# The router's sigmoid as ScalarE's own function, in place of an exponential, an addition and a reciprocal

## The chip, the cores and the metric

The kernel runs on one core of a Trainium2 chip. The metric is the device time of one execution in microseconds (us), as the median of the runs shown. The engines have short names in the profile: PE is TensorE (PEld its weight loads), DVE is VectorE, ACT is ScalarE, POOL is GpSimd, SP is SyncE, which here mostly issues DMAs.

## The reference

The input x has 16 rows of 256 time steps and 256 channels, 4096 tokens in all. First, spikes from a cumulative sum are added to it; then a mixture of experts with one shared expert is applied, with a residual. Cut to what matters:

```python
rates = relu(x) * 0.001
c  = cond[:, None, :] + cumsum(rates, axis=1)
x1 = x + (floor(c) - previous floor(c)) / 0.001      # a spike adds 1000

shared = (silu(xf @ w1) * (xf @ w3)) @ w2            # 256 -> 512 -> 256
s = sigmoid(concat([xf, tf]) @ router_W)             # tokens x 8 experts
_, topk_idx = top_k(s + router_bias, 2)
s_sel = take_along_axis(s, topk_idx)
gates = s_sel / (s_sel.sum() + 1e-9)
routed = sum over the two chosen experts of gates * (gelu(xf @ W1e) @ W2e)
out = x1 + (shared + routed) / 3
```

All arithmetic of weight is in fp32. The router's sigmoid `s` is used twice: to choose the two experts of each token, and for their gates.

## The kernel before

The 4096 tokens are cut into 8 chunks (`NCHUNK`) of 512 tokens (`N`), four sub-tiles (`J`) of 128 each. The kernel has three stages.

**Stage 1, by chunk.** For each chunk, `elementwise(i)` turns the input with PE transposes (tile `pt`), takes rates and a copy on ACT (L282, L291), and runs the cumulative sum on DVE (the scan at L306, sums at L316 to L321), the start value and the rounding on ACT (L334, L343), and the floor, difference and addition on DVE (L358 to L378). That gives the tile `x1`. One chunk later, `route(i)` computes the router of that chunk: 8 small matmuls into `pl` (L426), an addition on DVE (`lt`, L435), one transpose on PE into `pn` (L438), then the sigmoid: an exponential on ACT into the small tile `ex` (L442), an addition of 1 (L444) and a reciprocal (L445) on DVE into `sig`. About a dozen DVE operations on 128 x 32 elements follow: the bias, the best expert, the second best, and the sum `hot` of both choices (L447 to L470). PE counts with `hot` how many tokens went to each expert before (the tile `pr`, L475 to L480), then transposes `x1` back (`px`, L496); ACT copies that into the rows `x1t` (L497), DVE computes the target rows (`row`, `mine`, `at`, `at_i`, L502 to L509), and POOL scatters the rows to the expert regions in DRAM with 8 indirect DMAs (L513).

**The shared expert** is a stream of matmuls that fills PE in all stages: `shared_hidden` makes the tiles `ph` (L536), of which a pair gives one Silu on ACT (`as`, L546) and one product on DVE (`hs`, L547). The pool of `ph` has three buffers, so a fourth tile can be begun only when the Silu or the product has read the tile three before it. `shared_out` makes `pa` (L563) and adds it to `x1t` on DVE (L574). The helper `unit(n)` issues the next n tiles of this stream.

**Stage 2, by block.** After the last chunk, the rows are sorted by expert in DRAM. `run_blocks` takes 67 blocks (`MOST`) of 128 rows, loads each, turns it on DVE (L832), multiplies by the expert's weights on PE (`phe` L859, `py` L881) with a Gelu and a copy on ACT, and scatters the result on POOL (L890). Four further blocks run only if the counts need more than 67. **Stage 3** finishes the shared expert and combines.

**What sets the order.** Each engine works through its instructions in order. In the first and the last chunk's part, and in stages 2 and 3, regions marked `tc.manual_schedule` keep the order of the program on the engines they name. Between them, in the loop that runs `route(i - 1)` beside `elementwise(i)` for chunks 2 to 7, and for the router of chunk 0, the order on PE, DVE and ACT is chosen when the kernel is built, from the dependencies and the builder's own costs; so an edit in `route` also decides what stands around it. ACT's functions come in tables: an `ACT_TABLE_LOAD` stands in the instruction order wherever the next function isn't in the table that is active. After the first load, Relu, Identity and the copies have none of their own here; Silu, Gelu and the exponential do.

Of the kernel before, what the change touches and what calls it, by code (L numbers as in the profile page):

```python
# [16 lines left out]
AF = mybir.ActivationFunctionType  # L17
ALU = mybir.AluOpType
# [20 lines left out]
def kernel(  # L39
# [23 lines left out]
    nc = tc.nc  # L63
    B, T, D = x.shape
    HS = w1.shape[1]
    E, _, HE = w1e.shape
# [346 lines left out]
    def route(i):  # L413
        x1, x1t = x1s[i], x1ts[i]

        def small(tag, shape=(P, J, E), dt=F32):
            return rt.tile(list(shape), dt, tag=tag, name=f"{tag}_{i}")
# [18 lines left out]
        yield  # L436
        pn = p_t.tile([P, J, 32], F32, tag="pt", name=f"pn_{i}")
        nc.tensor.transpose(pn.rearrange("p j e -> p (j e)"), lt, ident)  # L438

        s = sig[:, ts(i, J), :]  # L440
        ex = small("ex")
        nc.scalar.activation(ex, pn[:, :, :E], AF.Exp, scale=-1.0)  # L442
        yield
        nc.vector.tensor_scalar(ex, ex, 1.0, None, ALU.add)  # L444
        nc.vector.reciprocal(s, ex)  # L445
        sel = small("sel")
        nc.vector.tensor_tensor(sel, s, rb[:, None, :].to_broadcast([P, J, E]), ALU.add)  # L447

# [214 lines left out]


    ro, nxt = route(0), elementwise(2)
    next(ro)
    next(ro)
# [17 lines left out]
    for i in range(2, NCHUNK):  # L685
        ro = route(i - 1)
        nxt = elementwise(i + 1) if i + 1 < NCHUNK else iter(())
        next(ro)
        next(el, None)
        unit()  # L690
        next(ro)
        next(el, None)
        next(ro)
        next(el, None)
        next(ro)
        unit()
        next(ro)
        next(el, None)
        next(ro)
        next(nxt, None)  # L700
        unit(1 + (i > 3 and i % 3 != 2) + (i == NCHUNK - 1))
        next(ro)
        next(el, None)
        next(ro)
        next(el, None)
        if i <= E // 2:
            load_experts(i - 1)
        el = nxt
    last = ctx.enter_context(ExitStack())
    last.enter_context(tc.manual_schedule(engines={PE, DVE, ACT}))  # L710
    nc.vector.tensor_copy(bidx, bidx_i)
    ro = route(NCHUNK - 1)
    next(ro)
    unit(0.5)
# [341 lines left out]
```

## Time and profile before

| what | value |
|---|---|
| median of the three runs | 335.84 us (335.32 to 845.69) |
| profiled execution, its own time | 334.36 us |
| its span, first to last instruction | 332.6 us |
| PE busy | 315.9 us, 95% of the span |
| DVE busy | 228.4 us, 69% |
| POOL busy | 164.8 us, 50% |
| ACT busy | 137.9 us, 41% |
| ACT table loads | 16: one at L282, 8 at L546, 6 at L442, one at L867, 1283 ns each |
| granted TensorE clock | 1.000 |

The span is shorter than the execution's own time by 1.76 us, which lie before the first and after the last instruction. The shares are averages over the three stages; stage 1 ends at about 142 us, where the last chunk's router is done, and there DVE is far busier than its average says. A line of the profile's groups gives the source line, the engine, the operation, the tile written and the tiles read, the count, the busy time with the mean of one in ns, and then the idle time of the engine just before, with what ended it.

### The profile page before, as it was taken

The page shows a single profiled execution, that of the slowest core. Times are in us where ns is not written, and L with a number is a line of the kernel's source. Part 1 is how long each engine was busy: PE and PEld are TensorE (multiplying, and loading weights), DVE is VectorE, ACT ScalarE, POOL GpSimd, SP SyncE. Part 2 cuts the span into 40 slices and gives each one's busy share as a digit, 9 for nine tenths or more (in the row PEclk, how much of TensorE's full clock was granted, in tenths as well). Part 3 has the DMA queues.
Part 4 walks back from the last instruction along what each step waited for, and adds up shares of the span by engine and source line. Part 5 has one row for each costly group of instructions (what it writes and reads, how often), then busy time and mean ns, then how long its engine had stood idle before and what let it go on. Part 6 is the DMA issues. An engine that isn't in the chain of part 4 may idle for free. (4 is left out here: it accounts for less than half of the span.)

```text
span 332.6 us, 6544 instructions
## 1 busy us (share of the span) xinstructions
PE 315.9 (95%) x1674; PEld 233.6 (70%) x1674; DVE 228.4 (69%) x656; ACT 137.9 (41%) x287; POOL 164.8 (50%) x197
## 2 busy tenths in 40 slices
PE   3799998999989999999999999999999999999996
PEld 2577644547545744746699999999999999465484
DVE  4777979999999997551477745554555552089993
ACT  4537385645675363040234344344444444301100
POOL 6000274787478688763035555555554655223220
PEclk9999999999999999999999999999999999999999
DMA  6999633242222212254446666666666762399933
GB/s 169 270 219 203 157 114 99 85 141 101 79 81 91 74 65 83 103 180 120 79 99 147 155 156 147 155 154 129 146 155 141 173 146 81 123 338 409 408 153 126
DMA packets 62533, 50.34 MB, mean 151 GB/s; under 512 B 42606, under 2 KB 52863, under 8 KB 62496
## 3 DMA queue, kind: packets, MB, share of 16 engines
q1 hardware_dynamic: 42240, 26.19, 32.7%
q0 software_dynamic: 7456, 20.86, 17.0%
q10 hardware_dynamic: 12800, 2.88, 5.2%
q8 instruction: 14, 0.23, 0.3%
q14 instruction: 23, 0.19, 0.2%
HBM read 27.44 MB, written 22.84 MB: 151 GB/s over the span
## 5 line engine op out<-in xcount | busy, mean ns | idle before, releaser
L536 PE MATMUL ph<-x,w_sb 128*128 128x512 f32 (+1 forms) x288 | 118.8, 559 | 4.8 <-DVE x L378 4.1
L890 POOL DMA_INDIRECT ys<-yb,to x67 | 66.1, 987 | 66.7 <-ACT yb L889 56.1
L513 POOL DMA_INDIRECT xs<-x1t,at_i x64 | 78.7, 1230 | 38.8 <-ACT xt L291 18.7
L536 PEld LDWEIGHTS ph<-x,w_sb 128*128 128x128 f32 x288 | 53.8, 195 | 53.2 <-issue 42.0
L859 PEld LDWEIGHTS phe<-xbt,w1e 128*128 128x128 f32 x536 | 70.3, 191 | 4.7 <-ACT hbt L867 0.9
L859 PE MATMUL phe<-xbt,w1e 128*128 128x128 f32 x536 | 70.7, 275 | 0.7 <-DVE xbt L832 0.7
L881 PE MATMUL py<-we,hbt 128*128 x268 | 68.8, 380 | 0.0
L827 DVE COPY w1e<-we 128x512 f32 x67 | 28.8, 430 | 45.2 <-PE phe L859 44.7
L563 PE MATMUL pa<-w_sb,hs 128*128 128x256 f32 x256 | 57.7, 380 | 0.0
L563 PEld LDWEIGHTS pa<-w_sb,hs 128*128 128x128 f32 x256 | 48.2, 190 | 8.9 <-issue 2.8
L881 PEld LDWEIGHTS py<-we,hbt 128*128 128x128 f32 x268 | 45.9, 191 | 3.5
L546 ACT ACTIVATE as<-ph 128x512 f32<-128x512 f32 (+1 forms) x36 | 19.9, 553 | 63.9 <-PE ph L536 54.1
L867 ACT ACTIVATE hbt<-phe 128x256 f32<-128x256 f32 x67 | 25.7, 383 | 45.2 <-PE phe L859 36.1
L547 DVE TENSOR_TENSOR hs<-as,ph 128x512 f32<-128x512 f32 (+1 forms) x36 | 22.4, 622 | 27.6 <-PE ph L536 21.4
L889 ACT COPY yb<-py 128x256 f32<-128x256 f32 x67 | 24.9, 372 | 22.7 <-PE py L881 21.8
L832 DVE STREAM_TRANSPOSE xbt<-xb 128x256 f32<-128x256 f32 x67 | 29.2, 436 | 0.0
L306 DVE TENSOR_TENSOR_SCAN tb<-keep,rates 128x1024 f32<-128x1024 f32 (+2 forms) x10 | 18.6, 1859 | 1.6 <-ACT rates L282 1.5
L497 ACT COPY x1t<-px 128x512 f32<-128x512 f32 x16 | 8.6, 591 | 25.1 <-PE px L496 25.1
L334 ACT ACTIVATE ta<-ta,cond_t 128x256 f32<-128x256 f32 x32 | 14.1, 498 | 7.9 <-DVE ta L321 7.0
L589 POOL DMA_DIRECT2D out_dram<-yc x8 | 5.8, 728 | 22.7 <-DVE yc L997 14.3
L463 POOL COPY x1t<-first 128x16 f32<-128x16 f32 x8 | 4.1, 516 | 22.6 <-DVE first L456 22.6
L574 DVE SCALAR_TENSOR_TENSOR x1t<-pa,x1t 128x512 f32<-128x512 f32 x14 | 9.6, 684 | 7.3 <-PE pa L563 7.3
(135 smaller groups left out, 264.5 us busy)
## 6 DMA issues: line engine op xcount, KB each, us to landing
xb<-xs SPq DMA_DIRECT2D x184, 33.0 KB
yc<-ys SPq DMA_DIRECT2D x8, 512.0 KB
we<-ys SPq DMA_DIRECT2D x8, 512.0 KB
xn<-in_x_dram SPq DMA_DIRECT2D x7, 512.0 KB
xb<-xs ACTq DMA_DIRECT2D x84, 33.0 KB
we<-in_L_cond_W1e_dram SPq DMA_DIRECT2D x8, 256.0 KB
we<-in_L_cond_W2e_dram SPq DMA_DIRECT2D x8, 256.0 KB
out_dram<-yc POOLq DMA_DIRECT2D x8, 256.0 KB, 6.2
```

The costliest lines, as they stand in the source:

```text
L513: nc.gpsimd.indirect_dma_start(out=xs_w[(i * J + j) * TOPK + q][:, :], out_offset=bass.IndirectOffsetOnAxis(ap=at_i[:, q, j : j + 1], axis=0),
L536: nc.tensor.matmul(ph, lhsT=w[:, k, ts(u, P)], rhs=x1[:, k, cols], start=(k == 0), stop=(k == KD - 1),)
L546: nc.scalar.activation(act, ps[0], AF.Silu)
L547: nc.vector.tensor_tensor(ht[:, u, cols], act, ps[1], ALU.mult)
L563: nc.tensor.matmul(pa[:, q, :], lhsT=ht[:, s, ts(n * h + q, P)], rhs=w2_sb[:, s, :], start=(s == 0), stop=(s == KS - 1),)
L827: nc.vector.tensor_copy(w, we[:, bass.ds(off, KD * HE)])
L832: nc.vector.transpose(xt.rearrange("p g k r -> p g (k r)"), block[b].pop("xb")[:, :, :FQ])
L859: nc.tensor.matmul(ph[:, m, :].rearrange("p (g r) -> p g r", r=Q), lhsT=w[:, k, ts(m, P)], rhs=xt[:, :, k, :], start=(k == 0), stop=(k == ...
L867: nc.scalar.activation(ht, ph, AF.Gelu)
L881: nc.tensor.matmul(py, lhsT=ht[:, k, :], rhs=we[:, bass.ds(off + KD * HE + k * D, D)], start=(k == 0), stop=(k == KH - 1),)
L889: nc.scalar.copy(yb, py)
L890: nc.gpsimd.indirect_dma_start(out=ys_w[b][:, :], out_offset=bass.IndirectOffsetOnAxis(ap=to[:, b : b + 1], axis=0), in_=yb, in_offset=Non ...
```

## The change

In `route`, the exponential with scale -1 into the small tile `ex`, the addition of 1 and the reciprocal are taken out. One ACT instruction with the function Sigmoid reads `pn` and writes the chunk's part of `sig`. The bias addition that follows on DVE then waits for ACT where it waited for the reciprocal. The `yield`, at which the router's steps are cut for interleaving, stands behind the ACT instruction as before. Lines below L446 move up by four.

```diff
         pn = p_t.tile([P, J, 32], F32, tag="pt", name=f"pn_{i}")
         nc.tensor.transpose(pn.rearrange("p j e -> p (j e)"), lt, ident)
-
         s = sig[:, ts(i, J), :]
-        ex = small("ex")
-        nc.scalar.activation(ex, pn[:, :, :E], AF.Exp, scale=-1.0)
-        yield
-        nc.vector.tensor_scalar(ex, ex, 1.0, None, ALU.add)
-        nc.vector.reciprocal(s, ex)
+        nc.scalar.activation(s, pn[:, :, :E], AF.Sigmoid)
+        yield
         sel = small("sel")
         nc.vector.tensor_tensor(sel, s, rb[:, None, :].to_broadcast([P, J, E]), ALU.add)
```

## The prediction

> **What bounds the kernel now.** I read the engines' busy time first, then the busy time by stretches of 20 us, then what PE waits for. The page's first lines:
>
> ```profile
> span 332.6 us, 6544 instructions
> ...
> PE 315.9 (95%) x1674; PEld 233.6 (70%) x1674; DVE 228.4 (69%) x656; ACT 137.9 (41%) x287; POOL 164.8 (50%) x197
> ```
>
> PE leaves 332.6 - 315.9 = 16.7 us free in the whole span, so no edit off PE can bring more than 5%. Where that time lies is seen in the view by stretches (length, then busy us of PE, PEld, DVE, ACT, POOL, each with its count; then clock and DMA):
>
> ```profile
> 20.00:40.00 20.00, 19.68 (x138) 14.95 (x137) 17.07 (x46) 11.46 (x23) 1.15 (x2) 1.00 0.94 173
> 40.00:60.00 20.00, 18.89 (x78) 9.01 (x77) 17.55 (x46) 13.39 (x21) 13.32 (x11) 1.00 0.37 124
> 60.00:80.00 20.00, 20.00 (x87) 11.18 (x86) 18.92 (x55) 12.02 (x22) 16.07 (x14) 1.00 0.35 115
> 80.00:100.00 20.00, 18.46 (x102) 10.95 (x100) 19.51 (x56) 11.86 (x22) 12.99 (x10) 1.00 0.24 80
> 100.00:120.00 20.00, 19.60 (x104) 12.57 (x104) 19.53 (x49) 9.82 (x17) 14.86 (x13) 1.00 0.21 75
> 120.00:140.00 20.00, 19.45 (x88) 11.86 (x87) 14.99 (x50) 6.87 (x12) 15.76 (x16) 1.00 0.25 90
> ...
> 200.00:220.00 20.00, 20.00 (x139) 18.84 (x138) 10.68 (x35) 8.55 (x23) 11.25 (x12) 1.00 0.66 149
> ```
>
> The router works only in the stretches from 20 to about 142 us. There DVE is up to 98% busy and PE idle for 0.32 + 1.11 + 0 + 1.54 + 0.40 + 0.55 = 3.92 us. From 180 to 280 us PE has no free time, so whatever is gained or lost in stage 1 shifts the rest as it stands. The waits of PE itself (who waited for whom: total us, times, longest):
>
> ```profile
> PE ph L536 <- DVE x L378: 4.1, 2, 3.6
> PE pt L275 <- DMA xn<-in_x_dram: 3.9, 1, 3.9
> PE pr L475 <- DVE hot L470: 2.9, 5, 0.9
> ```
>
> The first two are the start, before any router. The third is the end of the router's chain: `pr` waits for `hot`, five times. By the timeline these are chunk 1 at 51.86 us (0.90), chunk 3 at 83.68 (0.43), chunk 4 at 94.44 (0.63), chunk 5 at 112.67 (0.40) and chunk 6 at 123.43 (0.55): 2.91 us of the 3.92. So the chain that the edit shortens ends in a wait of the bounding engine, but in short waits.
>
> **The change part by part.** The groups that it removes or replaces, and, from the timeline, the chunk that shows the spacing best (start, duration, engine, line):
>
> ```profile
> L445 DVE RECIPROCAL sig<-ex 128x32 f32<-128x32 f32 x8 | 2.8, 351 | 0.2
> L444 DVE TENSOR_SCALAR ex<-ex 128x32 f32<-128x32 f32 x8 | 1.4, 175 | 5.6 <-ACT ex L442 5.6
> L442 ACT ACTIVATE ex<-pn 128x32 f32<-128x32 f32 x8 | 1.6, 197 | 4.1 <-PE pn L438 4.0
> L442 ACT ACT_TABLE_LOAD x6 | 7.7, 1283 | 0.1
> ```
>
> ```profile
> 45.79 0.18 DVE L444 TENSOR_SCALAR ex<-ex 128x32 f32<-128x32 f32 x1 [1.92 <-ACT ex L442]
> 46.01 0.35 DVE L445 RECIPROCAL sig<-ex 128x32 f32<-128x32 f32 x1
> 46.39 0.19 DVE L447 TENSOR_TENSOR sel<-sig,rb 128x32 f32<-128x32 f32 x1
> ```
>
> *Removed.* 8 additions and 8 reciprocals, 1.4 + 2.8 = 4.2 us of DVE. On the chain it is the spacing from the addition to `sel`: 46.39 - 45.79 = 0.60 us a chunk.
>
> *Replaced.* Sigmoid isn't in the trace. Its nearest rows are the 197 ns of the exponential in the same place, and from below the 185 ns of a 128 x 32 copy (L216); the pointwise functions on 128 x 512 all lie between 0.57 and 0.64 us, Silu among them. I take 197 ns: no difference. The other bound is worth 8 x 12 ns, nothing.
>
> *Added.* The changed kernel's instruction order has 20 table loads on ACT where the kernel before has 16. Before, the exponentials of chunks 4 and 6 followed those of chunks 3 and 5 with no Silu between, so they needed no load (6 at L442 for 8 exponentials). In the changed order a Silu of the shared expert (chunk 3's first, chunk 4's first) stands before the Sigmoid of chunks 4 and 6, with a load on each side of it: 2 loads for the Sigmoid and 2 more for Silu, 4 x 1.283 = 5.13 us of ACT. In the trace a load takes its 1.283 us and nothing around it: the one at 44.27 us is followed by the exponential at 45.56. ACT is busy for 11.86 and 9.82 of 20 us there, so the loads fit; the question is only what stands behind them.
>
> The Trainium skill (ScalarE: Activation LUTs, "What ACT_TABLE_LOAD costs") speaks against this change: it asks to batch activations by table set and prices each switch at 2.66 us, 1283 ns for the load and 1380 ns for a drain. The trace agrees on 1283 ns and shows no drain beside it; by the page the four switches would be an estimated 10.6 us of ACT in place of 5.13. Each switch would then be 1.38 us longer, the Silus behind the loads of chunks 4 and 6 would come some 1.6 us too late, and the sum below would be near +2.5 us instead of -1.9, an estimate too.
>
> *Moved.* The build chooses the order of stage 1 anew. Three patterns come out of the changed order; I work each with the durations of the trace.
>
> Chunk 1: `hot` is now interleaved with chunk 2's floor and spikes, 3 more large DVE operations of that chunk and one more product stand before it than in the old order, and ACT has the rounding (1.04 us) before the load and the second Silu. Following DVE's list from `sel` at 46.25 with 0.11 us for a small operation beside a large one and 0.22 us alone, `hot` is done at about 54.1 instead of 51.8. But PE has 3 more `ph` calls before `pr` (two rows of 0.43 us each, 2.6 us), so it arrives at 54.4 at the earliest: the wait of 0.90 is covered. Against it, the second Silu ends at 49.1 instead of 48.07, and the third `ph` buffer comes free that much later: about 1.0 us in which PE stops. Net 0.1 us lost; bounds 0.9 gained and 1.0 lost.
>
> Chunks 3 and 5: the router's chain runs first, the floor of the next chunk behind it, so `hot` comes at least 0.6 us earlier. PE has fewer `pa` calls before `pr`, the same work moved behind it. The waits of 0.43 and 0.40 go: 0.83 gained. If the next chunk's `x1` came late instead, PE would wait at `pl`; the same DVE work less 0.6 us stands before it, so that excludes more than a few tenths.
>
> Chunks 4 and 6, with the loads. Chunk 4 before:
>
> ```profile
> 87.08 2.29 DVE L306 TENSOR_TENSOR_SCAN tb<-keep,rates 128x1024 f32<-128x1024 f32 x1
> 87.53 0.27 PE L438 MATMUL pn<-ident,lt 128*128 128x128 f32 x1
> 87.84 0.20 ACT L442 ACTIVATE ex<-pn 128x32 f32<-128x32 f32 x1 [0.32 <-PE pn L438]
> 89.28 0.15 DVE L444 TENSOR_SCALAR ex<-ex 128x32 f32<-128x32 f32 x1
> 94.44 0.19 PE L475 MATMUL pr<-hot,before_b 128*128 128x32 bf16 x1 [0.63 <-DVE hot L470]
> ```
>
> The exponential ended at 88.04 and DVE read it only at 89.28, behind the scan: 1.24 us of cover. After, `lt` stands behind the scan, so `pn` comes at about 87.9; then Silu to 88.6, the load to 89.9, Sigmoid to 90.1. DVE needs until 90.2 for its sums and 90.85 for the product that now stands before `sel`, so the Sigmoid is not waited for, by 0.75 us. Thirteen small operations at 0.225 us put `hot` at 93.8. PE has half a `ph` tile (0.86 us) more before `pr` and arrives at 94.1: no wait. The load behind it ends the next Silu at 93.8 instead of 93.5, and its buffer is wanted only after `px`, at 95. So the wait of 0.63 goes, of which I count the chain's 0.60; chunk 6 has the same pattern, and its 0.55. Without that cover, each of the two chunks would lose one load, 1.28 us.
>
> Chunk 7 is in the order written by hand: `hot` was ready at 137.94 and `pr` ran at 140.86 behind `pa` and `ph`, so its 0.60 us hides behind 2.9 us of matmuls; chunks 0 and 2 had no wait worth counting.
>
> *Sum.* +0.1 - 0.83 - 0.60 - 0.55 = -1.9 us, rounded to -2.0, since some of PE's short stops lie inside its modelled ends (51.86 to 58.12 us holds about 0.8 us of them). The profiled execution's 334.36 us (332.6 us of span and 1.76 around it) becomes 332.4. The median of the runs lies 1.48 us above the profiled one, so the prediction for the median is 335.84 - 2.0 = 333.8 us. A measurement of this kernel tells about 2% from no change, 6.7 us; this is well inside it.
>
> **The rivals.** *The table loads reach PE.* Place: the Silu behind the second load in chunks 4 and 6, and the Sigmoid before it. For it: the margins of my working are 0.75 us and about 1 us, less than a load, and the `ph` pool has only three buffers. It decides once ACT is over 1.2 us late at those two Silus. Then one load a place and nothing gained elsewhere costs 2 x 1.28 = 2.6 us: 338.4 us. All four loads bare would be 5.13, 341.0, still under 2%. Against it: ACT is idle half of the time. Slower than before: 0.17.
>
> *PE's waits only move.* PE has 95% of work; a wait removed at `pr` turns up at `pl` (on `x1`), or at a `ph` buffer. For it: one such wait stands in the trace (`pl` waits 0.5 us for a Silu at 99.6), and the new order delays the second Silu of chunk 1. Time 335.8; 0.21.
>
> *DVE was the true pace of stage 1.* Its 19.5 of 20 us speak for it, PE's 20.00 between 60 and 80 against it. Then 7 chunks x 0.60 = 4.2 us come out: 331.6; 0.06.
>
> *It doesn't only do what it says.* A slightly different sigmoid could choose other experts and change the count of blocks. From the inputs, the second and third best score of a token are never closer than 0.0022, and the experts get 38, 3914, 161, 36 and 4043 choices, 67 blocks in all. If the four further blocks ran, that would be 4 x 1.73 us (139 matmuls in 20 us, 12 a block) = 6.9 us: 342.7; 0.01.
>
> **How the numbers follow.** The forecast has 0.55. Its own range is 332.5 (all of the 2.91 us, and a few tenths of hidden stops) to 335. Down to 331.0 it takes in the 3.92 us of all idle time in the stage, DVE's 4.2 us and half a microsecond between runs; up to 337.5 the rivals with waits moved and most of the case of loads on PE's path. Faster by over 2% needs 329.1 us, more than all the idle time of the stage: 0.03. Slower by over 2% needs 342.6, more than all four loads bare: 0.03.
>
> **What would show it.** Right: 16 DVE instructions fewer, 20 table loads, PE's wait for `hot` down from 2.9 us to under 1, and PE idle between 20 and 140 us down from 3.92 to about 2. Wrong: Silu waits at `ph` or waits for `x1` at `pl` that make up for it; a Sigmoid much over 200 ns, or a table load with idle time around it; a `phe` group that isn't x536.

## The result, and the profile after

The change makes the kernel 0.2% faster: 334.56 us median of 22 runs against 335.31 us of the kernel before, a ratio of 0.9981 with a 95% interval of 0.9971 to 0.9991, so 0.3 to 1.0 us. The forecast was a gain of 2.0 us, to 333.8 us; it started from 335.84, the median of the three runs shown then, which 22 runs bring to 335.31. The direction was right and the size a third of it; within the 2% there is no difference. The profiled execution took 334.05 us with a span of 332.3 (before 334.36 and 332.6). The page's first lines, as the ones shown of before:

```profile
span 332.3 us, 6527 instructions
...
PE 316.1 (95%) x1674; PEld 233.2 (70%) x1674; DVE 227.0 (68%) x640; ACT 143.6 (43%) x291; POOL 163.8 (49%) x197
```

DVE has its 16 instructions fewer, but is busy only 1.4 us less, not 4.2: that sum counted the busy time of operations that ran partly under their neighbours. (In the old order, run below with the Sigmoid, DVE is busy 225.6 us, 2.8 less than before; the other 1.4 us come with the new order.) ACT has 5.7 us more, of which the four added table loads are 4 x 1.283 = 5.13. The groups of the Sigmoid and of the loads (busy, mean ns | idle before, releaser):

```profile
L542 ACT ACT_TABLE_LOAD x10 | 12.8, 1283 | 0.5 <-ACTq L950 0.3
L440 ACT ACT_TABLE_LOAD x8 | 10.3, 1283 | 0.1
L440 ACT ACTIVATE sig<-pn 128x32 f32<-128x32 f32 x8 | 1.6, 197 | 4.8 <-PE pn L438 4.7
```

The Sigmoid takes the 197 ns that were assumed, a load the same 1283 ns with nothing idle around it. By stretches of 20 us:

```profile
20.00:40.00 20.00, 19.70 (x136) 14.66 (x135) 17.14 (x44) 11.36 (x22) 2.72 (x2) 1.00 0.91 182
40.00:60.00 20.00, 19.75 (x81) 9.97 (x80) 16.54 (x41) 12.89 (x21) 12.69 (x11) 1.00 0.36 110
60.00:80.00 20.00, 18.73 (x84) 10.55 (x83) 18.95 (x56) 12.66 (x23) 15.85 (x15) 1.00 0.34 115
80.00:100.00 20.00, 19.57 (x100) 11.37 (x99) 18.80 (x49) 14.52 (x24) 14.31 (x12) 1.00 0.28 94
100.00:120.00 20.00, 19.44 (x105) 11.69 (x104) 19.52 (x45) 11.32 (x18) 13.91 (x12) 1.00 0.17 62
120.00:140.00 20.00, 19.43 (x88) 11.94 (x87) 15.27 (x50) 8.16 (x13) 14.53 (x16) 1.00 0.28 103
```

PE's idle time from 20 to 140 us is 0.30 + 0.25 + 1.27 + 0.43 + 0.56 + 0.57 = 3.38 us, where it was 3.92. The stretch from 40 to 60 us won 0.86, that from 60 to 80, which had no idle time, lost 1.27. Of the waits and, from the timeline, where the longest lies:

```profile
PE pr L471 <- DVE hot L466: 2.5, 4, 1.3
```

```profile
65.17 0.19 PE L471 MATMUL pr<-hot,before_b 128*128 128x32 bf16 x1 [1.27 <-DVE hot L466]
```

The wait for `hot` fell from 2.9 us to 2.5, not to under 1. Those of chunks 1 and 4 are gone, chunk 2 has a new one of 1.27 us, chunk 3 keeps its 0.43, chunk 5 has 0.23 of 0.40, chunk 6 has 0.57 of 0.55.

**A ledger by chunk.** Waits at one line don't show what PE loses at others, and the page's busy time has modelled ends. So I took, from each trace, the time from one chunk's first `pr` matmul to the next, less the matmuls between them at full pace (0.427 us for a `ph` row of 512 columns, 0.214 for one of `pa`, 0.107 for a transpose, as they follow one another undisturbed in the trace, and 0.84 for a chunk's `pr` and `pl` together). What remains is PE time lost in that chunk, in us; c1 ends at chunk 1's `pr`. The rows below the first two belong to the experiments.

| kernel | c1 | c2 | c3 | c4 | c5 | c6 | c7 | sum |
|---|---|---|---|---|---|---|---|---|
| before | 1.74 | 1.30 | 1.28 | 1.26 | 1.90 | 1.27 | 0.23 | 8.98 |
| after | 1.47 | 1.73 | 1.26 | 0.81 | 1.33 | 1.85 | 0.29 | 8.74 |
| Sigmoid, old order | 1.57 | 1.22 | 0.83 | 1.19 | 1.69 | 1.19 | 0.24 | 7.93 |
| old form kept in odd chunks | 1.74 | 1.21 | 1.26 | 1.19 | 1.81 | 1.19 | 0.24 | 8.64 |
| old form kept in even chunks | 1.56 | 1.32 | 0.85 | 1.27 | 1.68 | 1.26 | 0.25 | 8.19 |
| unread pair behind `hot` | 1.98 | 1.63 | 1.05 | 1.47 | 2.16 | 1.85 | 0.24 | 10.38 |
| mixed order | 1.56 | 1.22 | 0.83 | 1.87 | 1.33 | 2.51 | 0.24 | 9.56 |
| old order, Silu as Sigmoid | 0.20 | 1.03 | 0.88 | 1.18 | 1.37 | 1.20 | 0.24 | 6.10 |
| new order, Silu as Sigmoid | 0.77 | 1.74 | 1.26 | 0.82 | 1.33 | 1.85 | 0.30 | 8.07 |
| chunk 1 old, then new order | 1.56 | 2.13 | 1.27 | 0.81 | 1.26 | 1.87 | 0.29 | 9.19 |
| old order, chunk 1's Sigmoid early | 0.63 | 1.50 | 0.89 | 1.20 | 1.68 | 1.19 | 0.23 | 7.32 |
| old order, chunk 1 in one go | 0.70 | 1.16 | 0.83 | 1.19 | 1.69 | 1.19 | 0.24 | 7.00 |
| `lt` and Sigmoid first | 1.48 | 1.75 | 1.32 | 1.64 | 1.41 | 2.76 | 0.29 | 10.65 |

The change is worth 0.24 us in this ledger, 0.31 us between the profiled executions and 0.6 between the runs. A row is one execution. Five of the experiments' kernels were profiled twice, and the two profiles agree within 0.07 us in every chunk but chunk 3 (in four kernels) and chunk 6 (in one), where one of the two executions had waits of its own; the last section comes back to those of chunk 3.

### The profile page after: what moved, and what is told of

Same layout as the page of the kernel before. It is cut to its first block, busy times and chain, and to the rows that moved or that the text cites. A ratio compares the mean times of both kernels' runs of the same rounds, so it can differ in the third digit from the quotient of the medians.

```text
span 332.3 us, 6527 instructions
## 1 busy us (share of the span) xinstructions
PE 316.1 (95%) x1674; PEld 233.2 (70%) x1674; DVE 227.0 (68%) x640; ACT 143.6 (43%) x291; POOL 163.8 (49%) x197
## 5 line engine op out<-in xcount | busy, mean ns | idle before, releaser
L509 POOL DMA_INDIRECT xs<-x1t,at_i x64 | 77.9, 1218 | 40.2 <-issue 16.8
L559 PE MATMUL pa<-w_sb,hs 128*128 128x256 f32 x256 | 58.8, 381 | 0.0
```

The source lines that it names most:

```text
L509: nc.gpsimd.indirect_dma_start(out=xs_w[(i * J + j) * TOPK + q][:, :], out_offset=bass.IndirectOffsetOnAxis(ap=at_i[:, q, j : j + 1], axis=0),
L559: nc.tensor.matmul(pa[:, q, :], lhsT=ht[:, s, ts(n * h + q, P)], rhs=w2_sb[:, s, :], start=(s == 0), stop=(s == KS - 1),)
```

## The experiments

The edit changes two things at once: the operations, and the order of stage 1 that the builder chooses. To part them, a helper records each PE, DVE and ACT instruction and ties it to its neighbour in a given list, so that any order can be built with any set of operations. In the profiles of these kernels nearly every line of stage 1 therefore bears the helper's number, L205 or L206. "Old order" and "new order" are the orders of the kernel before and of the changed kernel. Ratios are to the kernel before, timed beside each kernel.

**Sigmoid in the old order.**

```diff
-ex = exp(-pn); ex = ex + 1; s = 1 / ex
+s = sigmoid(pn)
 PE, DVE, ACT: old order
```

> The changed operations in the order of the kernel before: Sigmoid on ACT, no addition and reciprocal on DVE, and every PE, DVE and ACT instruction of stage 1 in the old order (16 table loads). Theory A (the newly built order took the gain back): the gain of the forecast appears, about -1.9 us, 333.4 us, ratio near 0.994, PE's wait for hot under 1 us. Theory B (PE sets the pace of stage 1 and a wait taken away at pr comes back at the next place, whatever the order): the same as the change as built, about -0.6 us, ratio 0.998, PE idle between 20 and 140 us still 3 us or more. Theory C (the four added table loads took it back): as under A, since this order has none of them.

Measured: 334.07 us, 0.9970 (0.9954 to 0.9985), about 1.0 us faster (0.5 to 1.5). So taking the operations out is worth about half of the forecast even with nothing moved. Its wait for `hot`:

```profile
PE pr L205 <- DVE hot L205: 1.9, 4, 0.7
```

Five waits shrank by 1.0 us together, not by 0.60 each. Chunk 4 shows why. DVE in the kernel before, behind the scan and the addition of 1 at 89.28, and the same place with the Sigmoid (start, duration):

```profile
89.40 0.21 DVE L316 COPY tot<-tb 128x60 f32<-128x60 f32 x1
89.53 0.34 DVE L445 RECIPROCAL sig<-ex 128x32 f32<-128x32 f32 x1
89.79 0.23 DVE L320 TENSOR_TENSOR_SCAN base<-keep,tot 128x64 f32<-128x64 f32 x1
89.94 0.16 DVE L447 TENSOR_TENSOR sel<-sig,rb 128x32 f32<-128x32 f32 x1
```

```profile
88.57 0.21 DVE L205 COPY tot<-tb 128x60 f32<-128x60 f32 x1
88.81 0.29 DVE L205 TENSOR_TENSOR_SCAN base<-keep,tot 128x64 f32<-128x64 f32 x1
89.02 0.17 DVE L205 TENSOR_TENSOR sel<-sig,rb 128x32 f32<-128x32 f32 x1
```

The big scan starts at 87.08 in the one and at 86.24 in the other, so `sel` comes 2.86 us behind it before and 2.78 us after. Only 0.08 us is saved: the addition stood in the tail of the big scan (the copy starts 2.32 and 2.33 us behind the scan's start, with and without it), and the reciprocal between a copy and a scan that waits for it: without it that spacing is still 0.24 us, not 0.39, and the one from the small scan to `sel` grows from 0.15 to 0.21. Even at chunk 1, where the 0.60 was read, `hot` starts only 0.19 us earlier (16.79 us behind chunk 0's `pr`, against 16.98): a product `hs` in the middle of the chain now waits 0.32 us for a Silu.

**The old operations in the new order.**

```diff
 ex = exp(-pn); ex = ex + 1; s = 1 / ex
-PE, DVE, ACT: old order
+PE, DVE, ACT: new order, addition and reciprocal just ahead of sel
```

> The exponential, the addition and the reciprocal put back, in the order that the build chose for the changed kernel (20 table loads). Theory A: the order alone costs about 1.3 us, so with the operations it is slower than before: 336.6 us, ratio 1.004. Theory B: between before and after, about 335 us, ratio 1.000. Theory C: the four loads cost 1.3 us, 336.6 us as under A.

Measured: 338.85 us, 1.0099 (1.0069 to 1.0129). Its wait for `hot` is 5.6 us, six times, 2.7 us more than before. The three runs at a clock of 1.000 took 337.58 to 338.15 us, which is that 2.7; the other three, at 0.995, took 339.54 to 339.98 (see the last section). The same removal is thus worth about 1 us in the old order and about 3 us in the new one, at the full clock: there is no price of the two operations by themselves.

**Where in the old order they cost.** The old form is kept in some chunks only, the order is the old one.

```diff
-s = sigmoid(pn)
+s = 1 / (exp(-pn) + 1) if i in (1, 3, 5) else sigmoid(pn)    # the other kernel: (2, 4, 6)
```

> The old order of instructions; chunks 1, 3 and 5 keep the exponential, the addition and the reciprocal, all other chunks take the sigmoid. With the sigmoid in all chunks this order ran in 334.07 us, 1.1 us under the old kernel. Theory 'gaps': in the even chunks the addition and the reciprocal lie between running sums that wait for one another, and their removal moved the sel addition up by only 0.08 us in chunk 4; nearly all of the 1.1 us comes from the odd chunks. Then this kernel is as slow as the old one, at most 0.3 us under it (ratio 0.999 to 1.000). Rival 'every chunk pays alike': half of the gain stays, 0.55 us under the old kernel (0.9984).

> The same with the old three operations kept in chunks 2, 4 and 6 and the sigmoid in all others. Theory 'gaps': the gain stays nearly whole, 0.8 to 1.1 us under the old kernel (ratio 0.9967 to 0.9976), and VectorE starts the sel addition of chunk 4 at most 0.2 us later than with the sigmoid. Rival 'every chunk pays alike': 0.55 us under the old kernel (0.9984), as with the odd chunks.

Beside these two the kernel before itself spread from 337.21 to 347.19 us; the ratios, 0.9965 (0.9912 to 1.0018) and 1.0037 (0.9984 to 1.0090), tell nothing. Both were measured again:

> The kernel with the old three operations in chunks 1, 3 and 5 once more, since in the first call the runs of every kernel, the old one's too, spread over 10 us. Theory 'gaps' (the removal pays in the odd chunks alone): at most 0.3 us under the old kernel. Rival 'every chunk pays alike': 0.55 us under it.

> The kernel with the old three operations in chunks 2, 4 and 6 once more, for the same reason. Theory 'gaps': 0.8 to 1.1 us under the old kernel. Rival 'every chunk pays alike': 0.55 us under it.

Measured: kept in the odd chunks 334.94 us, 0.9991 (0.9974 to 1.0007); kept in the even ones 334.57 us, 0.9979 (0.9965 to 0.9993). The middles (0.3 and 0.7 us under the old kernel) lean to the gaps, but the intervals hold both theories. The ledger parts them: with the old form in the odd chunks, chunks 1 and 3 lose what they lost before (1.74 and 1.26) and chunk 5 most of it (1.81; 1.90 before, 1.69 with the Sigmoid), and with it in the even chunks they lose what the Sigmoid leaves (1.56, 0.85 and 1.68). Removal gains 0.17, 0.45 and 0.21 us in chunks 1, 3 and 5, and 0.08, 0.07 and 0.08 in chunks 2, 4 and 6.

**The same work behind `hot`.** The old order and the Sigmoid, and on DVE two operations of the same shape whose result nobody reads.

```diff
 nc.vector.tensor_tensor(hot, hots[0], hots[1], ALU.add)
+nc.vector.tensor_scalar(spare, s, 1.0, None, ALU.add)
+nc.vector.reciprocal(spare, spare)
```

> The old order and the sigmoid in all chunks, but VectorE issues an addition and a reciprocal of the same shape, whose results nobody reads, directly behind the addition that makes hot. What VectorE has to do is as much as in the old kernel, but the two operations are no longer ahead of hot. Theory 'the chain to hot': what the old two operations cost was that they stood ahead of hot in the odd chunks; with them behind it the time stays near the 334.07 us of the same order without them, 0.7 to 1.1 us under the old kernel. Rival 'VectorE's load': the two operations cost what they take, wherever they stand, and the time is that of the old kernel, within 0.3 us.

> The kernel with two unread operations behind hot once more. Theory 'the chain to hot': 0.7 to 1.1 us under the old kernel. Rival 'VectorE's load': the old kernel's time within 0.3 us. The one profile of the first call speaks for the rival: from chunk 0's pr to the first matmul of the last stage it loses as much PE time as the old kernel.

The first measurement gave 1.0013 (0.9958 to 1.0068), beside the wide spread, the second 336.56 us, 1.0041 (1.0028 to 1.0053). Both theories missed: off the chain to `hot`, the two operations cost 2.5 us against the same order without them, more than twice what they cost ahead of it. Behind `hot` there is no gap, DVE goes from one operation to the next, and the next chunk's `x1` comes later each time; PE's wait for `hot` is 2.3 us and a wait of `pl` for `x` of 1.1 us stands beside it. At chunk 1, `hot` and the count `seen` that reads it start 1.14 us apart, where they start 0.72 apart without the pair: 0.42 us, and every chunk up to the sixth loses 0.22 to 0.66 more. So the sum of what DVE has to do paces these chunks too, and not the chain to `hot` alone.

**The Sigmoid ahead of the Silu, `lt` ahead of the scan.** The new order, changed in chunks 4 and 6 alone, where the prediction had feared the table loads.

```diff
 DVE:  +lt, then the 2.28 us scan, -lt
 PE:   +pn behind half of the next ph tile, -pn behind the whole
 ACT:  +Sigmoid, then Silu, -load, -Sigmoid, -load
```

> The changed kernel in its own order but for chunks 4 and 6: there lt stands ahead of the scan on DVE, the transposed logits come after half of the first ph tile on PE, and the Sigmoid stands ahead of Silu on ACT, which takes the four added loads away (16). Theory A in the narrow form (these two places took it back): about 1.2 us faster than the changed kernel, 333.4 us, ratio to before 0.994. Theory B: no difference to the changed kernel, ratio 0.998. Theory C: 333.4 us.

Measured: 336.85 us, 1.0048 (1.0026 to 1.0070), 2.3 us slower than the changed kernel. On DVE, `lt` in its new place stands still until PE has made `pl`, and the scan behind it waits too:

```profile
87.81 0.35 DVE L205 TENSOR_SCALAR lt<-pl,rc 128x128 f32<-128x128 f32 x1 [1.13 <-PE pl L205]
88.07 2.28 DVE L205 TENSOR_TENSOR_SCAN tb<-keep,rates 128x1024 f32<-128x1024 f32 x1
```

The scan starts 6.17 us behind chunk 3's `pr`, where it starts 4.70 behind it in the changed kernel, and `sel` 11.53 instead of 10.32. In chunk 6 the same wait is 0.73 us. The product `hs` and `sel` find the Silu and the Sigmoid done. So in the new order the scan had filled DVE's wait for `pl`: an engine's order was fitted to the others', and moving one step in it breaks the fit.

**Without table loads.** Silu becomes Sigmoid as well, so that one table serves all of stage 1; the hidden values are then others than the reference's. Four loads are left, where the new order has 20 and the old one 16.

```diff
-AF.Silu
+AF.Sigmoid
```

> The changed kernel in exactly its own order, with Sigmoid in place of Silu for the shared expert (the product with the argument is left out there, so its output is not the reference's; the router is untouched). ACT's functions of stage 1 then share one table and the loads between the Sigmoid and Silu fall away, all other instructions stay where they are. Theory C: the whole missing gain comes back and more, 333.3 us or less, ratio 0.994 or less. Theory A: the loads are mostly covered, a few tenths of a microsecond, 334.2 us, ratio 0.997. Theory B: no difference to the changed kernel, 0.998.

> The old order with the sigmoid in all chunks, and Sigmoid also in place of Silu for the hidden layer (other values come out), so that ScalarE loads 4 tables and not 16. In the new order the same edit took 20 loads down to 4 and the time from 334.56 to 333.58 us, 0.27% of the old kernel's. Theory 'the four added loads cost that': in the old order the loads lie beside PE's work, and the time stays at the 0.9970 of the old kernel that the same order had with them (0.9962 to 0.9978). Rival 'a pair of loads costs the same in both orders': 12 loads fewer bring 0.6 to 0.9 us, and the ratio is 0.9943 to 0.9952.

Measured: in the new order 333.58 us, 0.9954 (0.9937 to 0.9971); in the old order 331.73 us, 0.9888 (0.9868 to 0.9908). Leaving the loads out pays more in the old order than in the new one, by more than either theory had, so the four added loads are not what gives the gain back; the theory that they were fell. The ledger has no difference in chunks 4 and 6, where they stand (0.82 against 0.81, 1.85 against 1.85). Most of it lies at chunk 1: 1.57 against 0.20 in the old order, of 1.83 in all, and 1.47 against 0.77 in the new, which is all. The load there is one that both kernels have.

**Parts of one order, parts of the other.**

```diff
 mixed order:   old up to chunk 3's pr, new up to chunk 5's pr, then old
 chunk 1 old:   old up to chunk 1's pr, then new
 chunk 1 new:   new up to chunk 1's pr, then old
```

> The changed operations in a mixed order: the old order of the three engines up to chunk 3's pr, the changed kernel's order from there to chunk 5's pr, then the old order again. Theory: the new order loses PE time against the old one at chunks 2, 3 and 6 (about 0.5, 0.4 and 0.7 us by the working from the traces) and wins about 0.7 us over chunks 4 and 5, so the mix should take 0.3 to 0.7 us less than the sigmoid in the old order (334.07): 333.4 to 333.8 us, 1.4 to 1.8 us under the old kernel (ratio 0.9946 to 0.9958). Rival: the stretches don't add, since what one chunk wins is lost at the next seam; then 334 to 335 us (0.997 to 0.9995).

> The kernel in the mixed order once more. Theory: the stretches add, 1.4 to 1.8 us under the old kernel. Rival: what one chunk wins is lost at the next seam, 0.2 to 1.2 us under the old kernel.

> The changed operations, the three engines in the old order up to chunk 1's pr and in the changed kernel's order from there on. Theory 'chunk 1 gives back 0.7 us': in the changed kernel chunk 1's sigmoid with its table load stands ahead of ScalarE's sum of the threshold, which costs PE 0.7 us there; without it the time is 0.4 to 0.7 us under the changed kernel's 334.56 (ratio 0.9957 to 0.9969). Rival 'seams cost': the order cannot be cut, as in the mixed order; 334.6 us or more (0.998 or over).

> The changed operations, the three engines in the changed kernel's order up to chunk 1's pr and in the old order from there on. With the old order throughout the ratio was 0.9970, with the new one 0.9981. Theory 'chunk 1 gives back 0.7 us': the start of the new order alone loses what the whole one loses against the old order, and the ratio is 0.9980 to 0.9992. Rival 'the later chunks lose it': the ratio stays at 0.9970 (0.9962 to 0.9978).

Measured: the mixed order 0.9999 (0.9945 to 1.0053) beside the wide spread and 335.38 us, 1.0007 (0.9992 to 1.0021) the second time; chunk 1 old 335.41 us, 1.0000 (0.9983 to 1.0016); chunk 1 new 337.58 us, 1.0075 (1.0051 to 1.0100). No part added up. The mixed order does win chunk 5 (1.33 against 1.69) but pays 0.68 at the first seam and 1.32 in chunk 6, behind the second. With chunk 1 old, the new order pays 0.40 more in chunk 2 than it does by itself, and chunk 1 is no cheaper in the old order (1.56) than in the new (1.47). The last of the three made its own wait at the seam, shown in the last section, and says nothing on chunk 1. What an order is worth belongs to the whole of it.

**Chunk 1's load, moved.** The old order and the Sigmoid, and in chunk 1 only:

```diff
 ACT:  +Sigmoid (and its load), then 3 threshold activations, -Sigmoid, 1 more
 ACT:  second kernel also: +rounding tc, then load and Silu, -rounding tc
 DVE:  second kernel also: -hs in the middle of the chain, hot, +hs
```

> The changed operations in the old order, but in chunk 1 ScalarE issues the Sigmoid, and so its table load, ahead of the three threshold activations and not behind them. In the old order the load starts at 44.13 us, when pn has long been there, and VectorE stands still for 1.92 us ahead of sel. Theory 'the load at chunk 1 is what costs': the load runs in ScalarE's idle time ahead of pn, sel starts at about 43.8 and not at 45.65, and the truncated threshold is ready 0.35 us earlier; since hot waits for that too, the time falls by 0.2 to 0.5 us against the same order (ratio to the old kernel 0.9955 to 0.9964; the old order had 0.9970). Rival 'it is only a wait that moves': 0.9966 to 0.9978.

> The same, and the truncation of the threshold issued ahead of the next Silu and its load on ScalarE, and on VectorE the product of the hidden layer behind hot and not in the middle of the chain. Theory: hot is ready at about 48.5 us and not at 51.49, PE's wait of 0.72 us for it is gone, and the time is 0.7 to 1.2 us under the old order's (ratio 0.9934 to 0.9949). Rival: the product of the hidden layer, 0.65 us later, keeps its tile from PE, and what is won at hot is lost there; 0.996 or over.

> The kernel of the run before once more, since the old kernel's runs beside it spread over 8 us. Theory 'the load at chunk 1 is what costs': by the traces of stage 1 it loses 0.9 us less of PE's time than the same order without the move, so it should take 0.6 to 1.2 us less than that order's 334.07 us (ratio to the old kernel 0.9934 to 0.9952). Rival 'it is only a wait that moves': 0.9966 to 0.9978.

Measured: 0.9912 (0.9870 to 0.9954) for the first; for the second 0.9889 (0.9823 to 0.9956) and again 0.9948 (0.9904 to 0.9992). The kernel before spread over some 8 us beside them, so that the ratios show a gain and not its size. The traces show the place. ACT and DVE in the old order, where the load starts once the threshold is done, and then in the second kernel:

```profile
44.13 1.28 ACT L205 ACT_TABLE_LOAD   x1
45.42 0.20 ACT L205 ACTIVATE sig<-pn 128x32 f32<-128x32 f32 x1
...
45.65 0.19 DVE L205 TENSOR_TENSOR sel<-sig,rb 128x32 f32<-128x32 f32 x1 [1.92 <-ACT sig L205]
```

```profile
41.72 1.28 ACT L205 ACT_TABLE_LOAD   x1
43.01 0.20 ACT L205 ACTIVATE sig<-pn 128x32 f32<-128x32 f32 x1
...
43.49 0.18 DVE L205 TENSOR_TENSOR sel<-sig,rb 128x32 f32<-128x32 f32 x1
48.31 0.20 DVE L205 TENSOR_TENSOR hot<-chosen,chosen 128x32 bf16<-128x32 f32 x1
```

The load now runs while ACT has nothing to do, ahead of `pn`, and DVE's 1.92 us of standing still are gone. `hot` ends at 48.51 instead of 51.49. Chunk 1 loses 0.70 us of PE in place of 1.57 and nothing comes back later: the sum is 7.00, 2.0 us under the kernel before and 0.9 under the Sigmoid in the old order. The Sigmoid's move alone gets 0.6 of that (7.32). The second profile of the second kernel has the same 0.70 and 1.10 in chunks 1 and 2, but loses 4.67 in chunk 3, where PE stood still for 1.86 us and the clock fell. Two other kernels in the old order stopped there too when they were first measured, beside the wide spread (1.95 and 1.96 us), so this is hardly the move's doing. This is the best order found that computes the reference; that it beats the changed kernel, by how much at least, rests on the ledger of one execution each (8.74 against 7.00): the ratios, 0.9889 and 0.9948 against 0.9981, point the same way, but the second one's interval holds 0.9981.

## Why the prediction was right or wrong

**What held.** The bound (PE at 95%), the Sigmoid's 197 ns, 20 loads of 1283 ns with no drain beside them, the same 536 `phe` matmuls, a time well inside 2%. The new loads of chunks 4 and 6 are hidden, as the step said. The Trainium skill's price for a switch (ScalarE: Activation LUTs, "What ACT_TABLE_LOAD costs"), 1283 ns for the load and 2.66 us with a drain, agrees with these traces in the load and not in the drain: the next activation stands right behind the 1283 ns. Its rule to batch activations by set (same page, "Table sets: the hidden batching unit") would have paid at chunk 1 (0.20 us lost there in place of 1.57 in the old order without loads) and not at chunks 4 and 6 (no difference). The prediction's own lines show the 1.92 us that DVE stood still at chunk 1, but the sum has no term for it.

**The step that failed** is the gain at PE's waits for `hot`: 0.83 us for chunks 3 and 5 and 0.60 + 0.55 for chunks 4 and 6, with nothing for chunk 2. The sum took 0.60 us, or the whole wait, out of each place one by one. Against the ledger (after less before):

| chunk | forecast | measured |
|---|---|---|
| 1 | +0.1 | -0.27 |
| 2 | 0 | +0.43 |
| 3 and 5 | -0.83 | -0.02 and -0.57 |
| 4 and 6 | -1.15 | -0.45 and +0.58 |
| 7 | 0 | +0.06 |
| sum | -1.9 | -0.24 |

Of the 1.64 us that the sum missed, chunk 6 made 1.13, chunk 2 0.43, chunk 3 0.41 and chunk 4 0.15; chunks 1 and 5 gave 0.37 and 0.17 back. That chunk 4 came out near its 0.60 is in part luck, by the first of these points:

- *The price of the pair.* "The spacing from the addition to `sel`: 0.60 us a chunk" was read at chunk 1, where the three instructions stand alone. The forecast used it for chunk 4, whose own lines, shown in the same prediction, have the addition at 89.28 and would have shown `sel` at 89.94 with a copy and a scan in between. Measured in the old order, it is 0.07 to 0.08 us in the even chunks, 0.45 and 0.21 in chunks 3 and 5, and 0.17 at chunk 1 itself. All of them together are 1.05 us, where the sum took 1.98 out of the waits.
- *Chunk 3.* `hot` does come 2.6 us earlier (80.99 against 83.62), as the step had it. But the `pa` work that was "moved behind" had covered PE until then, so PE arrives earlier by as much and waits the same 0.43 us. A wait is a difference of two times, and the step worked out one.
- *Chunk 2* was passed over because it had no wait before. In the new order its router runs with fewer matmuls ahead of `pr`, and 1.27 us of waiting appears; the places where `pl` had been cut up by `ph` held most of the 1.30 us lost before, and with the 0.46 us lost beside the wait that leaves +0.43.
- *Chunk 6* was said to have "the same pattern" as chunk 4. It has the same order, but `lt`, behind the scan, starts 2.3 us later than before (118.09 against 115.76) and chunk 4's only 1.25; `sel` follows at 120.72 instead of 118.92, the wait for `hot` stays, and a new one of `pl` for the rates (0.33 us) comes ahead of it.
- *Chunk 1* came out better than worked: `hot` at 53.62 was worked as 54.1, the second Silu's end at 49.11 as 49.1, but PE lost little behind that Silu (one wait of 0.25 us, where about 1.0 was worked).

**The rivals.** That the table loads reach PE was wrong for the loads it named and right for one it didn't. That PE's waits only move is nearest to what happened: of the 1.05 us that the operations bring in the old order, the new order gives 0.81 back by the ledger (7.93 against 8.74). By the ratios, 0.9970 and 0.9981, it is about a third, and their intervals overlap. That DVE paces stage 1 has more to it than its 0.06: the unread pair behind `hot` cost 2.5 us, and the old pair in the new order about 3.

What stays open is why the builder's order loses in chunks 2 and 6 and wins in 4 and 5 in just these amounts: the three kernels that joined parts of both orders all paid at the seams and couldn't part it further.

## What to carry to other kernels

The price of an instruction on an engine's queue is what its neighbours leave of it: read the spacing in every place where it stands, and look for dependent neighbours whose gaps it fills. Where a builder chooses the order, an edit is two edits; run the new operations in the old order before crediting either. And work out a wait from both sides: what comes earlier for the engine that is waited for may come earlier for the one that waits.

## What the runs showed of the hardware

A stop of PE in stage 1 can cost twice. In six profiles PE stood still for 1.84 to 3.31 us at one place between 55 and 75 us, and in five of them the granted clock fell, around the end of the stop or up to 1.3 us behind it. The order with chunk 1 new has the longest stop:

```profile
60.39 0.44 PE L205 MATMUL pn<-ident,lt 128*128 128x128 f32 x1 [3.31 <-DVE tot L205]
```

```profile
60.00:65.00 5.00, 4.61 (x10) 2.87 (x11) 3.48 (x12) 1.66 (x3) 4.08 (x4) 0.66 0.25 90
```

A clock of 0.66 over 5 us is 1.7 us of PE. By stretches of 1 us it reads 0.53, 0.50, 0.50 and 0.77 from 60 to 64 us and 1.00 around them: the 1.70 us that are missing are those of a half clock held for 3.4 us. After stops of 1.84 us (the old operations in the new order) and of 1.86 to 2.00 us (three other profiles) the loss was the same 1.7 to 1.8 us, as 0.66 in one stretch of 5 us or 0.87 and 0.78 in two.

The sixth profile speaks against the length of the stop as the whole cause. With the old form in the even chunks, in the first measurement, PE stood still as long, ahead of the same `pl` of chunk 3 as in three of the five, and the clock stayed at 1.00:

```profile
73.51 1.14 PE L205 MATMUL pl<-x,rw 128*32 128x128 f32 x16 [1.95 <-DVE x L205]
```

```profile
75.00:80.00 5.00, 5.00 (x17) 2.72 (x16) 4.84 (x13) 3.32 (x7) 3.96 (x4) 1.00 0.24 84
```

After the 1.27 and 1.28 us of chunk 2, in the changed kernel and in the one with `lt` first, the clock stayed at 1.00 too, and so it did after the 3.6 us at the start of the kernel. What decides it, and that the stop is the cause at all, was not tested.
